# A graph layer's edge kernel: 52 instead of 42 edge tiles loaded row by row, half of each from ScalarE, and the result's rows sent a slot later

## The chip, the core and the metric

The kernel runs on one core of a Trainium2 chip. The metric is the device time of one launch in microseconds (us). The core's engines run their own instruction queues in order and wait for each other by semaphores: TensorE (PE), VectorE (DVE), ScalarE (ACT), GpSimd (POOL) and SyncE (SP). SyncE, ScalarE and GpSimd also start DMA transfers from their queues, in the order of the program.

## What is computed

One message-passing layer over 6250 nodes with 128 features and 206250 directed edges sorted by receiver, then a residual and a normalization. In float32, cut to what matters:

```python
def layer(node_feats, edge_feats, chi, cutoffs, senders, receivers):
    w = silu(edge_feats @ rad_W1 + rad_b1) @ rad_W2 + rad_b2       # 32 -> 128 -> 128
    w = w + silu(chi @ sph_W1 + sph_b1) @ sph_W2 + sph_b2
    q = (node_feats @ Wq)[receivers]; k = (node_feats @ Wk)[senders]
    v = (node_feats @ Wv)[senders]                                 # 8 heads of 16
    alpha = (q * w * k).sum(per head) / sqrt(16) * cutoffs
    return segment_sum(alpha * v, receivers) / 16
out = layernorm(x + layer(x, ...))
```

## The kernel before

**Tiles.** Edges are taken 128 at a time (a tile, one edge per partition). Four tiles make a quad (512 edges), four quads a group; there are 403 quads in 101 groups. The list `order` gives the quads of a group in the order 0, 2, 1, 3. The main loop makes one step per quad, called a slot here; `slot` runs from 0 to 3 in each group `g`, and `i` counts all slots. The program is one written order per engine: each engine works through its calls as the loop makes them.

**Set-up.** The keys and values of all nodes are computed once and stored as a table `kv_tab` (one row of 1 KB per node). The first ten quads don't use the table: their senders' features are gathered from x and multiplied. Meanwhile indices, receivers and biases are prepared.

**A slot.** On TensorE: small products of the group (`turn_q`, `make_q`, `sum_group`, lines 249 to 661), the sums of the group before (`sum_quads`, L616), the first layer of the quad after next (`first_layers`, L518), the queries at the edges of the next quad (`q_at_edges`, L527), and its second layer (`weigh`, L560 and L565). On ScalarE: the two silus of the quad after next (`silus`, L548), each held back by a mark of TensorE so that it does not run ahead, and one small copy out of PSUM (L253, L260, L652 or L661). On VectorE: query times key for the next quad (`multiply`, L577), and for the present one the product with the weights (L585), the sum per head (L587), the cutoff (L591) and the messages (L604). Per group VectorE also makes the one-hot matrices, of which `hotT` (L264) needs the receivers' indices `relb`; these are loaded by SyncE two groups ahead, in slot 2 (`load_rel`, L235), next to the edge features (`load_feats`, L224). `load_x` (L283) loads a piece of x in slot 0.

**Keys and values of an edge tile** come in one of two ways. Most tiles are fetched by GpSimd with one indirect DMA each (`gather`, L132), 14 quads ahead of their use into a ring of 16 buffers; a gather is held back by the mark of a quad of TensorE 14 quads earlier. In 42 quads, spread evenly from slot 20 to slot 392 (`row_at`), the fourth tile is instead loaded row by row into a buffer `wide` (three of them): 128 transfers of 1 KB, each with its address in a register. SyncE sends 80 of these rows in units of 32, 32 and 16: a register load (L186) and then a burst of rows (L191). ScalarE sends 48 in two units of 24, spread out: two rows between the two silus of a slot and up to four at its end. A register load of ScalarE stands at the end of a slot and takes the place of one row there. The window of a tile ends eight slots ahead of its use (`ROW_LEAD`). VectorE waits for a tile's rows in front of L577 (`multiply`), and handles the quad in two pieces, three tiles and one.

**The result.** Every fourth group, at the end of slot 3, `statistics` normalizes four pieces (ScalarE, L682 to L696, which needs another activation table and then silu's again) and puts them on a list `written`. `write_rows` (L708) in each slot sends one piece of the list from SyncE's queue, beginning with slot 0 of the next group. Pieces overlap in rows, so each write waits for the one before to land.

Of the kernel before, what the change touches and what calls it, by code (L numbers as in the profile page):

```python
# [35 lines left out]
NG = math.ceil(E / (P * GT))  # L36
# [9 lines left out]
ROW_BYTES = 2 * D * 4  # L46
XQ = 10
RING = 16
ROW_TILES = 42
ROW_FIRST = 20  # L50
ROW_LAST = 392
ROW_LEAD = 8
ROW_UNIT = 32
ROW_ACT = 48
ROW_UNIT_ACT = 24
ROW_SLOT_ACT = 6
ROW_SEMS = 8
CHECK = 20
XL = 3
# [6 lines left out]
def gnn_kernel(ctx, tc, x, src, dst, weight, edges, rad_W1, rad_b1, rad_W2, rad_b2,  # L66
# [26 lines left out]
    src_x = const.tile([P, math.ceil(XQ / NQ) * GT], I32, name="src_x")  # L93
    at_i = const.tile([ROW_TILES, P], I32, name="at_i")
    scale = const.tile([P, NT], F32, name="scale")
# [32 lines left out]
    def quad_of(name, bufs, width=D):  # L128
        return ep.tile([P, QT, width], F32, name=name, bufs=bufs)
# [8 lines left out]
    order = [g * NQ + j for g in range(NG) for j in (0, 2, 1, 3) if g * NQ + j < QUADS]  # L138
    row_at = [ROW_FIRST + (n + 1) * (ROW_LAST - ROW_FIRST) // ROW_TILES for n in range(ROW_TILES)]
    row_quads = {order[i] for i in row_at}  # L140
    row_of = {}
    row_done = {}
    act_rows, act_now = [], []
    row_sems = [tc.alloc_semaphore(f"rows_{n}") for n in range(ROW_SEMS)]
    row_count = [0] * ROW_SEMS

    def next_rows(n):
        for _ in range(min(n, len(act_now))):
            act_now.pop(0)()

    def rows_at_end():
        n = ROW_SLOT_ACT - 2
        m = min(n, len(act_now))
        next_rows(m)
        if not act_now and act_rows:
            f, e, r = act_rows.pop(0)
            act_now.extend(f(e, r))
            next_rows(n - m - 1)

    r_of = {}  # L160
    feats_of, relb_of, act_of, kv_of, hot_of, hotT_of, x_of, q_of, msg_of = ({} for _ in range(9))
# [11 lines left out]
    def load_rows(i):  # L173

        k = next((k for k in range(ROW_TILES) if i <= row_at[k] - ROW_LEAD), None)
        start = len(order) if k is None else (row_at[k - 1] if k else ROW_FIRST) - ROW_LEAD + 1
        if i < start:
            return rows_at_end() if k is None else None
        q = order[row_at[k]]
        n = P - ROW_ACT  # L180
        slots, units = row_at[k] - ROW_LEAD + 1 - start, math.ceil(n / ROW_UNIT)
        a, b = ((j * units + slots - 1) // slots for j in (i - start, i - start + 1))
        table = kv_tab.bitcast(U8).rearrange("(o n) b -> o (n b)", o=1)

        def registers(e, m, engine):
            return nc.values_load_multi_w_load_instructions(  # L186
                at_i[k:k + 1, e:e + m], engines=(engine,), min_val=0,
                max_val=(N - 1) * ROW_BYTES, skip_runtime_bounds_check_because="senders are nodes")[1]

        def one_row(engine, p, r):  # L190
            return engine.dma_start(row_of[q][p:p + 1, 0, :].bitcast(U8), table[:, ds(r, ROW_BYTES)])  # L191

        def rows_of_act(first, m):
            rows = registers(first, m, ACT)
            for p in range(m):
                yield lambda p=p: signalled(one_row(nc.scalar, first + p, rows[p]))

        def signalled(o):
            tc.no_tile_sem_insts.add(o.ins.name)
            tc.add_to_no_dep_group(f"rows_{q}", o.ins)  # L200
            o.then_inc(row_sems[k % ROW_SEMS], 16)
            row_count[k % ROW_SEMS] += 16
            row_done[q] = row_sems[k % ROW_SEMS], row_count[k % ROW_SEMS]

        if i == start:
            row_of[q] = quad_of("wide", 3, P)[:, :2, :].rearrange("p t d -> p (t d)")[:, None, :]
        for e in range(a * ROW_UNIT, min(min(b, units) * ROW_UNIT, n), ROW_UNIT):
            m = min(ROW_UNIT, n - e)
            rows = registers(e, m, SP)
            for p in range(m):  # L210
                signalled(one_row(nc.sync, e + p, rows[p]))
        if i == start:
            act_rows.extend((rows_of_act, e, min(ROW_UNIT_ACT, P - e)) for e in range(n, P, ROW_UNIT_ACT))
        rows_at_end()

    def kv_parts(q, t):

# [55 lines left out]
    def rows_from(table, at):  # L273

        return table.bitcast(U8).rearrange("n b -> (n b)")[ds(at, P * D * 4)].rearrange(
            "(p b) -> p b", p=P)
# [30 lines left out]
    with tc.tile_pool(name="nodes", bufs=1) as nodes, \  # L307
# [76 lines left out]

        rows_f = nodes.tile([P, ROW_TILES], F32, name="rows_f")

# [6 lines left out]
        def turn_rows():  # L393
            pt = nps.tile([P, QT, P], F32, name="pt", bufs=3)
            nc.tensor.transpose(pt[:ROW_TILES, 0, :], rows_f, ident)
            nc.vector.tensor_copy(at_i, pt[:ROW_TILES, 0, :])

# [64 lines left out]
        n = len(chunks)  # L462
# [49 lines left out]
    with tc.tile_pool(name="ps", bufs=1, space=PSUM) as pp:  # L512
# [192 lines left out]
        def write_rows(n=1):  # L705
            for _ in range(min(n, len(written))):
                g, y = written.pop(0)
                nc.sync.dma_start(rows_from(out, r_of.pop(g)), y.bitcast(U8))  # L708
# [16 lines left out]
        def verdict():  # L725

            pe = pp.tile([P, D], F32, name="po")
            nc.tensor.matmul(pe[:1, :8], ones[:, :1], ends, start=True, stop=True)
            found = gp.tile([1, 1], F32, name="found")
            nc.vector.tensor_reduce(found, pe[:1, :8], AX.X, OP.add)  # L730
            nc.vector.tensor_scalar(general, found, 0.0, None, op0=OP.is_gt)

        written = []
# [9 lines left out]
        multiply(order[0])  # L743
        marks = weigh(order[0])
        mark = marks[-1]
        for g in range(NG - 1):
            for slot, j in enumerate((0, 2, 1, 3)):
                q = g * NQ + j
                i = g * NQ + slot
                turned, past, old = None, mark, marks  # L750
                if slot == 0 and g == CHECK + len(checks) + 1:
                    verdict()
                if slot == 0:
                    turned = turn_q(g + 1, pp.tile([P, EQ], F32, name="pq", bufs=2))
                if slot == 1 and 2 <= g:
                    turned = sum_group(g - 2)
                if slot == 2:
                    turned = make_q(g + 1, pp.tile([P, EQ], F32, name="pq", bufs=2))
                if 1 <= g:
                    for t in ((), (0, 1), (2,), (3,))[slot]:  # L760
                        mark = sum_quads(g - 1, t)
                first_layers(order[i + 2])
                mark = q_at_edges(order[i + 1])
                marks = weigh(order[i + 1])
                silus(order[i + 2], mark, marks, lambda: next_rows(2))
                if turned:
                    turned()
                if 1 <= g and slot == 3:
                    part_sums(g - 1)
                if i + AHEAD < len(order):  # L770
                    gathers(order[i + AHEAD], old[-QT:])
                multiply(order[i + 1], mark)
                messages(q, scores(q, marks=marks), marks=marks)
                if slot == 0:
                    if g + XL < NG:
                        load_x(g + XL, past)
                if slot == 2:
                    if g + 3 < NG:
                        load_feats(g + 3, past)
                    if g + 2 < NG:  # L780
                        load_rel(g + 2)
                if slot == 1:
                    one_hots_T(g + 1)
                    if g + 2 < NG:
                        pick(g + 2)
                    if 1 <= g:
                        place(g - 1)
                write_rows()
                if slot == (3 if g < NG - 2 else 2):
                    if 2 <= g:  # L790
                        statistics(g - 2)
                if slot == 3:
                    if g + 1 < NG - 1:
                        one_hots(g + 1)
                    if CHECK <= g < CHECK + len(checks):
                        checks[g - CHECK]()
                if g == NG - 3 and slot in (0, 2):
                    wide_one_hots(order[slot // 2 - 3])
                if g == NG - 2 and slot == 0:
                    wide_one_hots(order[-1])  # L800
                    n = nc.values_load(general, min_val=0, max_val=1)
                    place(g)
                    place(NG - 1)
                if g == NG - 3 and slot in (1, 3):
                    weigh_wide(order[slot // 2 - 3])
                if g == NG - 2 and slot == 1:
                    weigh_wide(order[-1])
                load_rows(i)
# [206 lines left out]
```

## Time and profile before

| | |
|---|---|
| median of 3 runs | 1985.04 us (1985.03 to 1985.54) |
| profiled execution | 1985.41 us |
| its span, first to last instruction | 1983.3 us |
| granted TensorE clock, mean | 0.916 |
| instructions | 55295 |
| GpSimd gathers of kv_tab | 1530 |
| rows sent by SyncE / ScalarE | 3360 / 2016 |

The span leaves 2.1 us of the profiled execution outside. In the lines of the profile each group of instructions has its line, engine and operation, the tensors out<-in, and the count behind an x; behind the first bar stand the busy time (us) and the mean of one (ns), behind the second the engine's idle time in front of them and who ended it. In a timeline a row is start, duration, engine, line, operation and count, with the idle time in front of it in brackets. Busy time of a queue that only issues DMAs (SPq, ACTq) isn't in the busy shares of the engines. A row of windows has the window, its length, the busy time of each engine asked for (with the count of instructions), and at the end the granted clock, the busy share of the DMA engines and GB/s.

### The profile page before, as it was taken

The page shows a single profiled execution, that of the slowest core. Times are in us where ns is not written, and L with a number is a line of the kernel's source. Part 1 is how long each engine was busy: PE and PEld are TensorE (multiplying, and loading weights), DVE is VectorE, ACT ScalarE, POOL GpSimd, SP SyncE. Part 2 cuts the span into 40 slices and gives each one's busy share as a digit, 9 for nine tenths or more (in the row PEclk, how much of TensorE's full clock was granted, in tenths as well). Part 3 has the DMA queues.
Part 4 walks back from the last instruction along what each step waited for, and adds up shares of the span by engine and source line. Part 5 has one row for each costly group of instructions (what it writes and reads, how often), then busy time and mean ns, then how long its engine had stood idle before and what let it go on. Part 6 is the DMA issues. An engine that isn't in the chain of part 4 may idle for free.

```text
span 1983.3 us, 55295 instructions
## 1 busy us (share of the span) xinstructions
PE 1782.5 (90%) x16014; PEld 1505.7 (76%) x16014; DVE 1471.1 (74%) x3123; ACT 752.2 (38%) x1437; POOL 1488.6 (75%) x1580
## 2 busy tenths in 40 slices
PE   9899999978997988998898888899989988898897
PEld 7788788767876877876787777777767777777786
DVE  6687777768876877776777777767767767777777
ACT  3244344333343343342343333333433433433334
POOL 7777777777777777777777777777777777777775
PEclk9899899978998998998999889989989999898988
DMA  8545545455455555454554555545545455445543
GB/s 316 160 141 156 157 145 156 142 157 156 143 157 154 146 156 154 144 160 139 159 158 140 159 142 155 158 143 154 154 145 158 144 152 159 142 142 158 157 140 90
DMA packets 150194, 304.77 MB, mean 154 GB/s; under 512 B 38732, under 2 KB 83900, under 8 KB 149884
## 3 DMA queue, kind: packets, MB, share of 16 engines
q0 software_dynamic: 74720, 203.26, 36.7%
q1 hardware_dynamic: 69632, 95.45, 14.8%
q10 hardware_dynamic: 5532, 2.47, 0.5%
q8 instruction: 128, 2.10, 0.4%
q14 instruction: 182, 1.49, 0.3%
HBM read 287.58 MB, written 13.46 MB: 152 GB/s over the span
## 4 chain that ended last, share of the span: by engine, by line
PE 56%; DMA 17%; DVE 11%; issue 6%; POOL 3%; ACTq 2%; SPq 2%; ACT 2%; DVEq 0%; POOLq 0%
PE pw L565 28%; DMA kv<-kv_tab,src_i 14%; PE pq L527 10%; PE ph L518 7%; PE po L616 4%; DVE kq L577 4%; DMA relb<-rel_lin 3%; PE pw L560 3%; ACTq L191 2%; POOL msg L132 2%; DVE side L587 2%; DVE kq L585 2%; SPq L191 1%; PE pq L657 1%; POOL kv L132 1%
## 5 line engine op out<-in xcount | busy, mean ns | idle before, releaser
L132 POOL DMA_INDIRECT kv<-kv_tab,src_i x1530 | 1447.9, 946 | 466.6 <-PE pw L565 174.2
L548 ACT ACTIVATE act<-ph,b 128x512 f32<-128x512 f32 x806 | 546.5, 687 | 1091.0 <-PE pq L527 1003.5
L565 PEld LDWEIGHTS pw<-w,act 128*128 128x128 f32 x6448 | 822.8, 207 | 105.6 <-issue 94.7
L565 PE MATMUL pw<-w,act 128*128 128x128 f32 x6448 | 902.7, 298 | 0.0
L527 PE MATMUL pq<-q,hotT 32*128 32x128 f32 x3224 | 502.9, 299 | 50.8 <-DVE hotT L264 40.4
L518 PE MATMUL ph<-feats,w 32*128 32x512 f32 x1612 | 501.2, 680 | 31.5 <-ACT act L548 30.6
L527 PEld LDWEIGHTS pq<-q,hotT 32*128 32x128 f32 x3224 | 422.8, 200 | 75.9 <-issue 55.4
L577 DVE TENSOR_TENSOR kq<-pq,kv 128x512 f32<-128x512 f32 (+1 forms) x403 | 271.8, 674 | 243.8 <-PE pq L527 121.2
L587 DVE TENSOR_REDUCE side<-kq 128x32 f32<-128x512 f32 x403 | 280.1, 695 | 43.2 <-DVE kq L585 1.4
L604 DVE TENSOR_TENSOR msg<-kv,side 128x512 f32<-128x512 f32 (+1 forms) x404 | 271.9, 673 | 42.7 <-DVE side L591 1.2
L585 DVE TENSOR_TENSOR kq<-pw,kq 128x512 f32<-128x512 f32 x403 | 274.7, 682 | 0.0
L518 PEld LDWEIGHTS ph<-feats,w 32*128 32x128 f32 x1612 | 137.9, 193 | 113.7 <-issue 58.2
L560 PE MATMUL pw<-brow,onesb 3*128 3x512 bf16 x403 | 161.9, 402 | 9.4 <-DVE kq L585 9.3
L616 PE MATMUL po<-msg,hot 128*32 128x128 f32 x3200 | 154.6, 290 | 0.0
L264 DVE TENSOR_TENSOR hotT<-relb,side 128x512 f32<-128x512 bf16 x101 | 69.0, 683 | 97.5 <-DMA relb<-rel_lin 97.4
L657 PE MATMUL pq<-part,to 128*128 128x128 f32 x200 | 45.9, 313 | 82.6 <-DVE kq L577 58.0
L591 DVE TENSOR_TENSOR side<-side,scale 128x32 f32<-128x32 f32 x400 | 80.0, 200 | 42.3 <-DVE side L587 0.5
L657 PEld LDWEIGHTS pq<-part,to 128*128 128x128 f32 x200 | 31.3, 197 | 93.0 <-issue 54.0
L616 PEld LDWEIGHTS po<-msg,hot 128*32 128x32 f32 x3200 | 71.3, 111 | 38.3 <-issue 4.8
L269 DVE TENSOR_TENSOR hot<-rel,side 128x512 f32<-128x512 f32 x100 | 66.1, 661 | 0.0
L258 PE MATMUL pq<-wq,xT 128*128 128x128 f32 x200 | 42.9, 299 | 11.2 <-DVE kq L577 11.1
L132 POOL DMA_INDIRECT msg<-in_x,src_x x40 | 38.9, 972 | 13.3 <-issue 11.6
(117 smaller groups left out, 855.6 us busy)
## 6 DMA issues: line engine op xcount, KB each, us to landing
wide<-kv_tab SPq DMA_DIRECT2D x3360, 1.0 KB
feats<-in_edges SPq DMA_DIRECT2D x101, 512.0 KB
wide<-kv_tab ACTq DMA_DIRECT2D x2016, 1.0 KB
kv<-kv_tab,src_i POOLq DMA_INDIRECT x1530
relb<-rel_lin SPq DMA_DIRECT2D x101, 128.0 KB
x<-in_x SPq DMA_DIRECT2D x101, 64.0 KB
out<-y SPq DMA_DIRECT2D x101, 64.0 KB
kv_tab<-kv SPq DMA_DIRECT2D x12, 512.0 KB
```

Source lines behind the costliest of these rows:

```text
L132: return nc.gpsimd.indirect_dma_start(out=o, out_offset=None, in_=table, in_offset=bass.IndirectOffsetOnAxis(ap=index, axis=0))
L518: return nc.tensor.matmul(act_of[q, i], w1[r0:r0 + R, :], feats_of[g][r0:r0 + R, c0:c0 + EQ], start=True, stop=True)
L527: o = nc.tensor.matmul(pq_of[q][:, t, :], hotT_of[g][b, t * P:(t + 1) * P], q_of[g][b, :], start=True, stop=True)
L548: o = nc.scalar.activation(act, act_of[q, i], AF.Silu, bias=b1[:, i:i + 1])
L560: nc.tensor.matmul(pw, onesb, brow.rearrange("p t d -> p (t d)"), start=True, stop=False)
L565: o = nc.tensor.matmul(pw[:, t, :], act_of[q, i][:, t * P:(t + 1) * P], w2[:, i, :], start=False, stop=(t == QT - 1 and i == 1))
L577: o = nc.vector.tensor_tensor(kq_of[q][:, u, :], pq_of[q][:, u, :], kv[:, :, :D], op=OP.mult)
L585: nc.vector.tensor_tensor(m, pw_of[q][:, t, :], m, op=OP.mult)
L587: o = nc.vector.tensor_reduce(alpha, m.rearrange("p t (h e) -> p t h e", e=HD), AX.X, OP.add)
L604: o = nc.vector.tensor_tensor(msg_of[q][:, u, :].rearrange("p t (h e) -> p t h e", e=HD), kv[:, :, D:].rearrange("p t (h e) -> p t h e", e ...
L616: o = nc.tensor.matmul(po_of[g][j * W:(j + 1) * W, :], hot_of[g][:, j * QT + t, :], msg_of[g * NQ + j][:, t, :], start=(t == 0), stop=(t = ...
L657: nc.tensor.matmul(ph[:, :D], to[:n, 0, :], part[:n, :], start=True, stop=(g == 0))
```

## The change

The fourth tile of 52 quads is loaded row by row, over the same stretch of slots, so one quad in 7.15 has such a tile instead of one in 8.86. Each of the two engines sends 64 rows of a tile in two units of 32. ScalarE still sends two rows between the silus; at the end of a slot it now sends as many as bring it to an even share of the tile's rows over the slots of its window, and loads registers when it runs out of them, however many rows that makes. `write_rows` sends a piece only if the list already held something when the slot before had sent its own, so the first piece goes out in slot 1 instead of slot 0; the last two groups are as before.

```diff
-ROW_TILES = 42
+ROW_TILES = 52
...
-ROW_ACT = 48
-ROW_UNIT_ACT = 24
-ROW_SLOT_ACT = 6
+ROW_ACT = 64
+ROW_UNIT_ACT = 32
...
+    act_sent = [0]
 
     def next_rows(n):
         for _ in range(min(n, len(act_now))):
             act_now.pop(0)()
-
-    def rows_at_end():
-        n = ROW_SLOT_ACT - 2
-        m = min(n, len(act_now))
-        next_rows(m)
-        if not act_now and act_rows:
-            f, e, r = act_rows.pop(0)
-            act_now.extend(f(e, r))
-            next_rows(n - m - 1)
+            act_sent[0] += 1
+
+    def rows_at_end(goal):
+        while act_sent[0] < goal:
+            if not act_now:
+                f, e, r = act_rows.pop(0)
+                act_now.extend(f(e, r))
+            next_rows(min(len(act_now), goal - act_sent[0]))
...
         if i < start:
-            return rows_at_end() if k is None else None
+            return
...
-        rows_at_end()
+        rows_at_end(k * ROW_ACT + ROW_ACT * (i - start + 1) // slots)
...
         mark = marks[-1]
+        made_before = 0
         for g in range(NG - 1):
...
-                write_rows()
+                write_rows(1 if made_before or g >= NG - 2 else 0)
+                made_before = len(written)
```

## The prediction

> **What bounds the kernel now.** I began with busy time and the costliest groups, where GpSimd (POOL) looks a quarter idle.
>
> ```profile
> PE 1782.5 (90%) x16014; PEld 1505.7 (76%) x16014; DVE 1471.1 (74%) x3123; ACT 752.2 (38%) x1437; POOL 1488.6 (75%) x1580
> L132 POOL DMA_INDIRECT kv<-kv_tab,src_i x1530 | 1447.9, 946 | 466.6 <-PE pw L565 174.2
> DMA  8545545455455555454554555545545455445543
> ```
>
> It is not idle. 1447.9 + 466.6 = 1914.5 us, and 1914.5 / 1530 = 1.251 us per gather: 0.946 busy and 0.305 in front of it. The timeline of POOL at both ends shows that this gap is the same everywhere, whoever is named behind the arrow, so it belongs to the gather and is no wait for work.
>
> ```profile
> 52.87 0.94 POOL L132 DMA_INDIRECT msg<-in_x,src_x  x1 [0.30 <-issue]
> 54.12 1.03 POOL L132 DMA_INDIRECT kv<-kv_tab,src_i  x1 [0.30 <-DVE b_all L379]
> ```
>
> ```profile
> 1966.14 0.94 POOL L132 DMA_INDIRECT kv<-kv_tab,src_i  x1 [0.30 <-PE pw L565]
> 1967.39 0.94 POOL L132 DMA_INDIRECT kv<-kv_tab,src_i  x1 [0.30 <-issue]
> ```
>
> From 54.12 to 1968.33 POOL issues one gather behind the other; 1983.3 - 1968.3 = 15.0 us of tail follow. So the span is 54.1 + 1914.2 + 15.0. TensorE must keep up with this. How the two stand to each other I read from the windows of line 560 (one bias product opens each quad) and of line 132:
>
> ```profile
> 0.00:110.00 110.00, 4.40 (x11) 1.01 (x11) 0.94 0.69 226
> 110.00:980.00 870.00, 75.01 (x188) 17.46 (x188) 0.92 0.52 151
> 1020.00:1890.00 870.00, 72.70 (x180) 16.63 (x180) 0.92 0.52 151
> ```
>
> ```profile
> 0.00:110.00 110.00, 81.34 (x85) 0.94 0.69 226
> 110.00:980.00 870.00, 658.02 (x696) 0.92 0.52 151
> ```
>
> At 110 us POOL has done 45 kv gathers (85 less the 40 of x), which with the ten quads that need none makes about 21 quads; TensorE has begun 11. It starts ten quads behind, goes on at 870/188 = 4.63 us a quad, POOL feeds one per 4.86 (four gathers less a tenth), and near 980 TensorE has caught up. From there it is held at 870/180 = 4.83. The waits of VectorE before and after 980 us (two answers) say what holds it in each half:
>
> ```profile
> DVE hotT L264 <- DMA relb<-rel_lin: 82.1, 21, 12.3
> ```
>
> ```profile
> DVE kq L577 <- DMA kv<-kv_tab,src_i: 83.5, 54, 3.7
> DVE hotT L264 <- DMA relb<-rel_lin: 15.3, 5, 7.6
> ```
>
> First half: the receivers' load (relb), late because SyncE (SP) is behind; second half: the gathers. The end is set by the gathers alone.
>
> **The change part by part.** *Ten gathers fewer.* A tile loaded singly takes one gather off POOL. 52 - 42 = 10, times 1.251 us, is 12.5 us off a queue without slack: 1985.41 - 12.5 = 1972.9 for the profiled execution, 1985.04 - 12.5 = 1972.5 for the median, which lies 0.4 below it. Nothing late moves in behind, if TensorE keeps the new pace. It has 392 quads to begin between 110 us and where its last one may start:
>
> ```profile
> 1970.75 0.38 PE L560 MATMUL pw<-brow,onesb 3*128 3x512 bf16 x1
> ```
>
> To begin there 12.5 us earlier it may take (1958.2 - 110)/392 = 4.715 us a quad on its own; break-even is (1970.7 - 110)/392 = 4.747. It has 4.63 now, so 0.085 a quad, 33 us in all, may be lost before the gain shrinks, and 46 before it is gone. All other terms are weighed against these two.
>
> *ScalarE's queue* gets 3328 rows for 2016, and 104 register loads of 32 for 84 of 24. Per slot that is 64/7.15 = 8.9 rows instead of 5.4: two between the two silus as before, about seven behind instead of four. What stands behind them on the queue is the next quad's first silu; TensorE waits for that at the next first layer (line 518).
>
> ```profile
> 698.79 0.69 ACT L548 ACTIVATE act<-ph,b 128x512 f32<-128x512 f32 x1 [2.22 <-PE pq L527]
> 699.52 0.69 ACT L548 ACTIVATE act<-ph,b 128x512 f32<-128x512 f32 x1
> 700.26 0.55 ACTq L191 DMA_DIRECT2D wide<-kv_tab  x2
> 701.10 0.70 PE L518 MATMUL ph<-feats,w 32*128 32x512 f32 x2
> 701.63 0.59 PE L518 MATMUL ph<-feats,w 32*128 32x512 f32 x2
> 702.40 0.69 ACT L548 ACTIVATE act<-ph,b 128x512 f32<-128x512 f32 x1 [2.02 <-PE pq L527]
> 708.53 0.23 ACTq L191 DMA_DIRECT2D wide<-kv_tab  x1
> ```
>
> A row takes 0.55 - 0.23 = 0.32 us. In this slot, one of the short ones (3.6 us), the queue is done at 700.81 and the next silu comes at 702.40: 1.6 us to spare. Three more rows leave 0.65, so the ordinary slot costs nothing. A slot with a register load is another matter:
>
> ```profile
> L186 SPq TENSOR_LOAD <-at_i x126: 979/1924/2497, 122.9 to 1877.2; - x126
> L186 ACTq TENSOR_LOAD <-at_i x84: 1662/1780/2070, 127.0 to 1871.1; - x84
> ```
>
> ScalarE's 24 took 1.78; 32 did not occur there. Bounds: 1.8, and SP's longest (its 32s) 2.5. Scaled by 32/24 it is 2.4, which I take, with 0.2 for a first row behind it: 0.65 - 2.6 makes the silus 1.95 us late. First layers start 701.10 - 699.48 = 1.6 us behind the first silu's end, and the second pair 701.63 - 700.21 = 1.4 behind the second's, so TensorE loses about 0.55. Short slots are the rule; three silus in a row:
>
> ```profile
> 682.39 0.69 ACT L548 ACTIVATE act<-ph,b 128x512 f32<-128x512 f32 x1 [1.99 <-PE pq L527]
> 686.00 0.69 ACT L548 ACTIVATE act<-ph,b 128x512 f32<-128x512 f32 x1 [2.03 <-PE pq L527]
> 689.51 0.69 ACT L548 ACTIVATE act<-ph,b 128x512 f32<-128x512 f32 x1 [1.94 <-PE pq L527]
> ```
>
> They lie 3.6 and 3.5 us apart. I take three of a group's four slots (the one of the statistics is longer) to be that short while the clock is full; a mean clock of 0.92 with halves means full for about 0.83 of the time. 104 x 0.75 x 0.83 = 65 slots, 36 us. Bounds: nothing, if loads fall on long slots, and 104 x 0.65 = 68.
>
> *The statistics slots.* There rows stand between the normalizing and the reload of silu's table.
>
> ```profile
> 707.89 0.55 ACTq L191 DMA_DIRECT2D wide<-kv_tab  x2
> 708.99 0.48 ACT L696 ACTIVATE y<-y,shift,rs 128x128 f32<-128x128 f32 x1
> 709.49 1.28 ACT L548 ACT_TABLE_LOAD   x1
> 711.52 1.80 PE L518 MATMUL ph<-feats,w 32*128 32x512 f32 x2 [1.13 <-ACT act L548]
> ```
>
> TensorE already waits here, so lateness counts in full. Seven rows end at 707.83 + 7 x 0.32 = 710.1 instead of 709.1, past the last normalizing at 709.47: 0.6 us. With a load and seven to nine rows it is 3.2 to 3.8. In the changed kernel's queue 23 such slots carry rows, 7 of them a load (now 5, with fewer rows, worth about 1.3 each): 16 x 0.6 + 7 x 3.4 - 5 x 1.3 = 27 us; bounds 10 and 45.
>
> *SP's queue.* 64 rows per 7.15 slots instead of 80 per 8.86: 8.95 a slot for 9.03, still in bursts.
>
> ```profile
> 677.52 0.55 SPq L235 DMA_DIRECT2D relb<-rel_lin  x1
> 680.68 10.73 SPq L191 DMA_DIRECT2D wide<-kv_tab  x32
> 692.17 0.37 SPq L283 DMA_DIRECT2D x<-in_x  x1
> ```
>
> One burst with its load holds the queue from 678.1 to 691.4, nearly four short slots, so what queues behind (x, features, relb) comes late as now. The result's rows wait in the same queue; SP's waits in 100 to 980 us and TensorE's share of the relb waits there (two answers):
>
> ```profile
> SPq L708 <- DMA out<-y: 56.8, 22, 4.8
> SPq L708 <- ACT y L696: 5.4, 2, 5.0
> ```
>
> ```profile
> PE pq L527 <- DVE hotT L264: 35.6, 9, 9.2
> ```
>
> Two writes stood together ahead of a group's relb, the second waiting 56.8/22 = 2.6 us for the first to land. One slot later only one stands ahead; the pair, and its wait, moves behind relb, ahead of x and a burst. So relb gains 0 to 2.6 us in each of some 25 groups, and SP's total falls by nothing to 62 us in that half. I take part of it: relb no later than now.
>
> *Sum for TensorE.* 36 + 27 = 63 us over 392 quads is 0.16, so 4.79 if every relb wait stayed. But those waits are SP being slower than TensorE: 35.6/188 = 0.19 a quad at a pace of 4.63, and hardly any at 4.83 (15.3 us after 980, where SP had the same rows to send). What ScalarE adds takes their place first. With none left it is 4.60, with half of them 4.69; both are under 4.715. One more thing speaks for the second half of this exchange: the row of a long wait, and the window of all engines around it (granted clock: the third number from the end).
>
> ```profile
> 614.28 0.69 DVE L264 TENSOR_TENSOR hotT<-relb,side 128x512 f32<-128x512 bf16 x1 [10.30 <-DMA relb<-rel_lin]
> ```
>
> ```profile
> 614.00:618.00 4.00, 2.88 (x11) 2.36 (x12) 3.50 (x8) 0.69 (x1) 3.09 (x4) 0.50 0.55 129
> ```
>
> Behind the wait the clock is half, so a wait costs more than its length. The Trainium skill (TensorE: Matmul & The Clock Gate, Part 1) says that an idle window of about 3.4 us halves the matrix clock until a busy one has passed; the trace agrees, with 0.50 granted in the window right behind a 10.30 us wait for relb.
>
> *Small things.* All rows of a tile are still sent eight slots ahead of its use, so VectorE's wait for them stays met. VectorE does two products in two pieces for ten more tiles: twenty more instructions in an engine that is a quarter idle. Ten more one-column products and ten more rows of a transpose fall in the set-up, under TensorE's lag of ten quads: nothing.
>
> **Rivals.** (1) *Gathers still set the end:* 1972.5. For it: no slack anywhere on POOL. (2) *TensorE keeps part of the gain:* 4.715 to 4.747 a quad, 1972.5 to 1985; half of the relb waits stay and ScalarE costs its middle value or a little more. (3) *ScalarE's queue becomes the bound, slower:* the late silus of the load and statistics slots cost 63 us and the relb waits stay, since SP still sends bursts of 32. 4.79 x 392 + 110 = 1988 for the last quad instead of 1970.7: 17 us more, 2002. It decides from 46 us of new waits on. Against it: the two kinds of wait replace one another. (4) *No change:* the DMA engines are the limit, and it doesn't matter who sends the bytes. Then 1985. The busy share of 0.52 in the windows above, and gathers that start every 1.25 us whatever else flows, speak against it. The Trainium skill (DMA: Bandwidth & Descriptors, Issuing engines are not separate DMA queues) says just this of bandwidth, and that other issuers save only issue time; here issue time on POOL is what is short.
>
> **How the numbers follow.** (1) 0.77, (2) 0.08, (3) 0.12, (4) 0.03. Predicted: 1972.5. Its own range is 1970.5 to 1976: 2 us either way for how TensorE stands to the last gathers in the tail, a little more above for a denser row traffic. To hold 8 in 10 it takes in about half of (2): 1970.5 to 1981. A measurement here tells 0.2%, 4 us, from nothing. Faster: (1) and most of (2), 0.84; same: (4) and the end of (2), 0.04; slower: (3), 0.12.
>
> **What would show it.** Right: 1520 gathers still 1.25 us apart, the last one ending near 1956, the tail 15 us; relb waits smaller in total, a longer total of "PE ph from ACT act", kv waits of VectorE still in the second half. Wrong: gaps of more than 0.31 us in front of gathers (POOL waiting for TensorE's marks, which lie 14 quads back), TensorE never reaching the gathers and no kv waits at the end, or hotT waits above 100 us.

## The result: slower, 2003.2 us instead of 1985.0

The changed kernel takes 2003.16 us (median of 5 runs, 2001.40 to 2008.36) against 1985.03 for the kernel before on the same chip (1984.36 to 1985.54): a ratio of 1.0095, 95% interval 1.0081 to 1.0110. The prediction was 1972.5, faster. The profiled execution took 2001.40 us; its page begins (in the changed file the lines behind `ROW_ACT` stand one lower than before: L132 is now L131, L560 is L559, and so on):

```profile
span 1999.6 us, 57805 instructions
PE 1812.9 (91%) x16014; PEld 1516.8 (76%) x16014; DVE 1471.7 (74%) x3153; ACT 747.8 (37%) x1437; POOL 1479.0 (74%) x1570
```

The busy shares hardly differ from before. What differs stands in the costliest groups and at the end of the timeline of GpSimd, and then of TensorE:

```profile
L131 POOL DMA_INDIRECT kv<-kv_tab,src_i x1520 | 1438.5, 946 | 464.2 <-PE pw L564 172.0 <-issue 154.4 <-DMA kv<-kv_tab,src_i 63.5
...
1955.24 0.95 POOL L131 DMA_INDIRECT kv<-kv_tab,src_i  x1 [0.30 <-issue]
...
1986.60 0.38 PE L559 MATMUL pw<-brow,onesb 3*128 3x512 bf16 x1
```

Ten gathers fewer, still (1438.5 + 464.2) / 1520 = 1.252 us apart, the last one done at 1956.2: this half of the forecast came true to half a microsecond. But the last quad's bias product starts at 1986.60, where 1958.2 was needed, and POOL has long been done. From 110 us on TensorE needed (1986.6 - 110) / 392 = 4.787 us a quad. The windows of that product show the pace in both halves (the number in the first brackets of a row is the count of quads):

```profile
110.00:980.00 870.00, 72.12 (x180) 16.86 (x180) 0.92 0.53 150
1020.00:1890.00 870.00, 71.82 (x179) 16.87 (x179) 0.92 0.53 151
```

870/180 = 4.83 in the first, where it was 4.63, and 4.86 in the second, now without ever reaching the gathers. The clock is the same 0.92, and the DMA engines' busy share is 0.53 for 0.52. What VectorE, TensorE and SyncE wait for, in the whole run, first before:

```profile
DVE hotT L264 <- DMA relb<-rel_lin: 97.4, 26, 12.3
DVE kq L577 <- DMA kv<-kv_tab,src_i: 85.9, 58, 3.7
...
PE ph L518 <- ACT act L548: 30.6, 22, 2.6
...
SPq L708 <- DMA out<-y: 122.7, 50, 5.5
```

Then in the changed kernel (SyncE's row follows below):

```profile
DVE hotT L263 <- DMA relb<-rel_lin: 121.3, 29, 10.9
PE ph L517 <- ACT act L547: 93.4, 80, 5.0
...
DVE kq L576 <- DMA kv<-kv_tab,src_i: 10.7, 13, 1.3
```

The kv waits that marked the gathers as the bound (85.9 us in all before) are nearly gone. The waits for silus grew from 30.6 us to 93.4. The waits for relb grew from 97.4 to 121.3. SyncE's own list has what is in front of relb on its queue:

```profile
SPq L707 <- DMA out<-y: 195.8, 56, 11.4
```

Before, SyncE waited 122.7 us in 50 waits for a written piece to land, so that the next piece may follow; the longest was 5.5. In 100 to 980 us alone it is 87.6 for 56.8. One such wait in SyncE's timeline:

```profile
423.37 10.85 SPq L190 DMA_DIRECT2D wide<-kv_tab  x32
434.32 0.37 SPq L223 DMA_DIRECT2D feats<-in_edges  x1
434.80 0.57 SPq L234 DMA_DIRECT2D relb<-rel_lin  x1
435.54 10.67 SPq L707 DMA_DIRECT2D out<-y  x2
446.93 0.35 SPq L282 DMA_DIRECT2D x<-in_x  x1
```

The first write of the pair goes out at 435.54, behind the 512 KB of edge features and relb. A transfer's landing is told by sixteen signals. The trace has fifteen of this write's: fourteen of them were there at 440.54, the last came at 445.75. SyncE stood still for 9.8 us and sent nothing.

**SyncE is the bound.** To see it, SyncE's time between the bias products of quads 10 and 200 is divided among its instructions (sums of their durations with the gaps under 0.15 us behind them, by 190 quads; us a quad):

```
                        before  changed  old writes  one write  few ScalarE rows  56/72 rows
pace of TensorE          4.648   4.790     4.788       4.617         4.590          4.682
rows sent                2.921   2.883     2.863       2.914         2.895          2.540
register loads for rows  0.629   0.606     0.605       0.591         0.616          0.544
waits at the writes      0.327   0.531     0.548       under 0.02    0.286          0.463
waits for TensorE        0.052   0.040     0.041       0.394         0.061          0.392
```

(The four columns on the right are experiments below.) Before, SyncE had 0.05 us a quad to spare in this half; in the changed kernel 0.04. What the rows leave of the pace, 0.72 to 0.74 us in every column, are SyncE's other loads. From before to changed the rows and loads fall by 0.06 as forecast, the waits at the writes rise by 0.20, and the pace by 0.14, which is their sum. In the second half (quads 200 to 385) the changed kernel goes on at 4.840.

### The profile page after: what moved, and what is told of

It reads as the page before. It is cut to its first block, busy times and chain, and to the rows that moved or that the text cites. A ratio compares the mean times of both kernels' runs of the same rounds, so it can differ in the third digit from the quotient of the medians.

```text
span 1999.6 us, 57805 instructions
## 1 busy us (share of the span) xinstructions
PE 1812.9 (91%) x16014; PEld 1516.8 (76%) x16014; DVE 1471.7 (74%) x3153; ACT 747.8 (37%) x1437; POOL 1479.0 (74%) x1570
## 2 busy tenths in 40 slices
DMA packets 152294, 304.94 MB, mean 152 GB/s; under 512 B 39852, under 2 KB 86300, under 8 KB 151964
## 4 chain that ended last, share of the span: by engine, by line
PE 60%; ACTq 9%; issue 8%; DMA 7%; DVE 7%; ACT 6%; POOL 2%; SPq 1%; DVEq 0%; POOLq 0%
PE pw L564 29%; PE pq L526 11%; PE ph L517 11%; ACTq L190 7%; ACT act L547 4%; DMA relb<-rel_lin 4%; PE po L615 4%; DMA kv<-kv_tab,src_i 3%; PE pw L559 2%; ACTq L185 2%; POOL msg L131 2%; DVE kq L576 2%; DVE side L586 1%; DVE kq L584 1%; PE pq L257 1%
## 5 line engine op out<-in xcount | busy, mean ns | idle before, releaser
L131 POOL DMA_INDIRECT kv<-kv_tab,src_i x1520 | 1438.5, 946 | 464.2 <-PE pw L564 172.0
L517 PE MATMUL ph<-feats,w 32*128 32x512 f32 x1612 | 552.8, 666 | 95.0 <-ACT act L547 93.4
L526 PE MATMUL pq<-q,hotT 32*128 32x128 f32 x3224 | 497.0, 296 | 59.2 <-DVE kq L576 59.0
L526 PEld LDWEIGHTS pq<-q,hotT 32*128 32x128 f32 x3224 | 417.4, 198 | 76.0 <-issue 75.2
L517 PEld LDWEIGHTS ph<-feats,w 32*128 32x128 f32 x1612 | 159.5, 191 | 218.6 <-ACT act L547 160.6
L559 PE MATMUL pw<-brow,onesb 3*128 3x512 bf16 x403 | 161.0, 400 | 0.0
L263 DVE TENSOR_TENSOR hotT<-relb,side 128x512 f32<-128x512 bf16 x101 | 69.0, 683 | 121.4 <-DMA relb<-rel_lin 121.3
L131 POOL DMA_INDIRECT msg<-in_x,src_x x40 | 38.6, 966 | 13.3 <-issue 11.6
```

The lines of the kernel that those rows point to most:

```text
L131: return nc.gpsimd.indirect_dma_start(out=o, out_offset=None, in_=table, in_offset=bass.IndirectOffsetOnAxis(ap=index, axis=0))
L517: return nc.tensor.matmul(act_of[q, i], w1[r0:r0 + R, :], feats_of[g][r0:r0 + R, c0:c0 + EQ], start=True, stop=True)
L526: o = nc.tensor.matmul(pq_of[q][:, t, :], hotT_of[g][b, t * P:(t + 1) * P], q_of[g][b, :], start=True, stop=True)
L559: nc.tensor.matmul(pw, onesb, brow.rearrange("p t d -> p (t d)"), start=True, stop=False)
```

## Experiments

Every ratio is against runs of the kernel before on the same chip. The first eight ran on chips where that kernel takes 1988.6 (the first four) and 1984.7 us (the next four).

**Writes in their old place.** Is it the slot by which the writes were put off?

```diff
-                write_rows(1 if made_before or g >= NG - 2 else 0)
+                write_rows()
```

> The changed kernel with the result's rows sent as before (first piece in slot 0). Theory A (SyncE: the second write of a pair now waits behind features and relb, so relb comes late): SyncE's waits for out fall from 196 us to about 125, VectorE's relb waits from 121 us to 80 or less, and the time to 1978-1988. Theory B (ScalarE: late silus behind the added rows and register loads): relb waits may fall, but the first layer's waits for silu rise above their 93 us instead, and the time stays at 1997-2003.

Measured: 2003.26 us, ratio 1.0064 (1.0047 to 1.0081). SyncE's waits at the writes and VectorE's for relb:

```profile
SPq L707 <- DMA out<-y: 182.0, 54, 6.8
SPq L707 <- ACT y L695: 62.8, 11, 26.2
```

```profile
DVE hotT L263 <- DMA relb<-rel_lin: 133.2, 35, 11.3
```

The theory that the new place of the writes is the cause falls. Back in front of relb the writes wait as long for each other to land: 0.51 us a quad in the stretch of the table above, for 0.50 in the changed kernel and 0.30 before. For ScalarE they wait 0.04 to 0.05 in all three. The ratio is 0.3% below the changed kernel's, but so much slower was the kernel before on this chip, and the changed kernel wasn't run on it: a gain of that size is not excluded.

**One write a group.** Pieces of the result go out four slots apart, so that none waits for the one before.

```diff
-                write_rows(1 if made_before or g >= NG - 2 else 0)
+                write_rows(1 if slot == 2 or g >= NG - 6 else 0)
```

> The changed kernel with one piece of the result sent per group, in slot 2 behind relb (each slot again in the last five groups), so that no write finds the one before still under way. Theory A: SyncE's waits for out under 30 us, relb waits under 40 us, time 1972.5-1978 (the gathers' bound). Theory B: 1993-2003, the first layer's waits for silu at 93 us or more.

Measured: **1978.19 us, ratio 0.9949 (0.9932 to 0.9965)**, faster than both kernels. The waits of SyncE, TensorE and VectorE in this run:

```profile
SPq L707 <- DMA out<-y: 22.9, 9, 6.0
...
PE ph L517 <- ACT act L547: 83.6, 69, 5.0
...
DVE kq L576 <- DMA kv<-kv_tab,src_i: 93.8, 61, 6.7
```

The writes' waits are nearly gone, the relb waits wholly (they are no longer in VectorE's list), and the kv waits are back: the gathers set the end. ScalarE's late silus are nearly as many as in the changed kernel, 83.6 us. So they alone don't cost the gain; the theory that ScalarE's queue is the bound falls with this run.

**ScalarE's rows as two transfers.** The 64 rows of each tile that ScalarE sends become two transfers of 32 fixed rows, sent at the start of the tile's window (`next_units` sends all that is listed); the bytes are the same, the data are not the senders' rows.

```diff
...
-            rows = registers(first, m, ACT)
-            for p in range(m):
-                yield lambda p=p: signalled(one_row(nc.scalar, first + p, rows[p]))
+            yield lambda: signalled(nc.scalar.dma_start(
+                row_of[q][first:first + m, 0, :], kv_tab[first:first + m, :]))
...
-        rows_at_end(k * ROW_ACT + ROW_ACT * (i - start + 1) // slots)
+        if i == start:
+            next_units()
```

> The changed kernel with ScalarE's 64 single rows of a tile and their register loads replaced by two transfers of 32 fixed rows of the table (so these edges get wrong keys and values); SyncE as in the changed kernel. Theory A: SyncE stays late, relb waits stay at 100 us or more, time 1992-2003. Theory B: the first layer's waits for silu fall to 20 us or less and the time to 1972.5-1980.

Measured: 1973.99 us, ratio 0.9928 (0.9911 to 0.9945). The silu waits of TensorE and SyncE's waits at the writes:

```profile
PE ph L523 <- ACT act L553: 17.6, 22, 2.5
...
SPq L713 <- DMA out<-y: 96.1, 41, 5.6
```

Not only ScalarE's part falls, from 93.4 to 17.6. The waits of SyncE for its writes halve too, though SyncE's own list of work is untouched.

**SyncE's rows as two transfers.** The same for SyncE's 64 rows.

```diff
-            rows = registers(e, m, SP)
-            for p in range(m):
-                signalled(one_row(nc.sync, e + p, rows[p]))
+            signalled(nc.sync.dma_start(row_of[q][e:e + m, 0, :], kv_tab[e:e + m, :]))
```

> The changed kernel with SyncE's 64 single rows of a tile and their register loads replaced by two transfers of 32 fixed rows (these edges get wrong keys and values); ScalarE as in the changed kernel. Theory A: relb waits vanish, time 1972.5-1980. Theory B: relb waits vanish too, but the late silus remain and the time stays above 1988.

Measured: 1974.21 us, ratio 0.9931 (0.9914 to 0.9947).

```profile
PE ph L515 <- ACT act L545: 85.5, 65, 5.0
...
DVE kq L574 <- DMA kv<-kv_tab,src_i: 99.3, 62, 6.8
```

With SyncE relieved, 85.5 us of late silus remain and the gathers set the end all the same. This is the second run against ScalarE as the bound.

**56 rows from SyncE, 72 from ScalarE.** A theory formed from these runs: SyncE is full, and whatever takes work or waits off it helps, at ScalarE's cost if need be.

```diff
-ROW_ACT = 64
-ROW_UNIT_ACT = 32
+ROW_ACT = 72
+ROW_UNIT_ACT = 24
```

> The changed kernel with 56 rows of a tile from SyncE and 72 (three loads of 24) from ScalarE. Theory S (SyncE is full, and its work per slot, waits for out included, sets the pace): eight rows fewer per 7.15 slots take 0.36 us off SyncE's 4.79 us a slot, so the gathers bound again: 12 us below the kernel before, about 0.994 of it, relb waits under 60 us. Theory B (ScalarE's late silus cost TensorE directly): more rows on ScalarE, slower than the changed kernel, 1.010 of the kernel before or more.

Measured: 1980.22 us (1973.47 to 1981.47), ratio 0.9970 (0.9954 to 0.9986).

```profile
PE ph L517 <- ACT act L547: 137.2, 111, 4.8
...
1958.14 0.38 PE L559 MATMUL pw<-brow,onesb 3*128 3x512 bf16 x1
```

The silu waits grow to 137.2 us, 44 more than in the changed kernel, and yet the ratio is 0.9970 instead of 1.0095. In the profiled run (1973.47) the last quad starts at 1958.14, just where ten gathers fewer needed it.

**ScalarE's loads in units of 16.** Shorter loads, so shorter lateness for each.

```diff
-ROW_UNIT_ACT = 32
+ROW_UNIT_ACT = 16
```

> The changed kernel with ScalarE's registers loaded in four units of 16 instead of two of 32, so that no slot gets more than about 1.2 us of load. Theory S: the first layer's waits for silu fall to about half, but SyncE's waits for out and relb's lateness stay: 1.004 to 1.010 of the kernel before. Theory B: the time falls with those waits, to 1.000 or less.

Measured: 1999.83 us, ratio 1.0072 (1.0057 to 1.0086).

```profile
PE ph L517 <- ACT act L547: 69.9, 41, 4.0
...
SPq L707 <- DMA out<-y: 187.6, 56, 11.1
...
DVE hotT L263 <- DMA relb<-rel_lin: 137.0, 27, 12.7
```

The silu waits fall by 23.5 us, the relb waits rise by 15.7, the time stays within 4 us. While SyncE is full, a wait taken from ScalarE's side comes back at relb.

**The kernel before with one write a group.** The edit of the second experiment, made in the kernel before.

> The kernel before (42 tiles) with one piece of the result sent per group, in slot 2. Theory S: SyncE gets idle time, relb waits fall from 97 us to under 20, the first half runs faster, but the gathers set the end: 0.999 to 1.001. If relb waits had cost time in the kernel before: 0.997 or less.

Measured: 1986.23 us, ratio 1.0008 (0.9994 to 1.0022).

```profile
SPq L708 <- DMA out<-y: 11.6, 7, 2.2
...
DVE kq L577 <- DMA kv<-kv_tab,src_i: 163.1, 96, 4.5
```

SyncE's waits are nearly gone here too, and VectorE waits longer for the gathers instead (163.1 us for 85.9). Fewer writes in a row are worth nothing by themselves, and the ten gathers fewer, as the change makes them, cost 1%; together they are worth half a per cent.

**58 tiles with one write a group.** Six gathers fewer again.

```diff
-ROW_TILES = 52
+ROW_TILES = 58
```

> 58 tiles, 64 and 64 rows, one piece of the result per group. Theory S: SyncE's work is 4.26 us a slot at 52 tiles with this and rises by 0.4 to 4.7, still under the gathers' 4.81: six gathers fewer, 7.5 us below the kernel with 52 tiles and one write a group, 0.991 of the kernel before. If SyncE or ScalarE bind first: 0.995 or more, with relb waits back above 60 us.

Measured: 2025.47 us, ratio 1.0202 (1.0187 to 1.0217). It is not SyncE this time: its waits for writes are 22.1 us. The gathers of GpSimd are no longer evenly spaced:

```profile
391.77 0.95 POOL L131 DMA_INDIRECT kv<-kv_tab,src_i  x1 [0.30 <-DMA kv<-kv_tab,src_i]
...
400.53 0.95 POOL L131 DMA_INDIRECT kv<-kv_tab,src_i  x1 [0.30 <-issue]
403.93 0.95 POOL L131 DMA_INDIRECT kv<-kv_tab,src_i  x1 [2.45 <-PE pw L564]
405.21 0.94 POOL L131 DMA_INDIRECT kv<-kv_tab,src_i  x1 [0.33 <-issue]
```

104 starts lie over 1.4 us apart (two in the changed kernel), which adds 63 us. Gathers signal on eight semaphores in turn, and in such a gap GpSimd waits for the one of the gather eight before. The gather at 403.93 is eight behind the one at 391.77, which had fifteen of its sixteen landing signals at 395.21 and the sixteenth at 403.17, 0.76 us ahead of that start. (The arrow names TensorE, whose mark only came last by the profile.) In 90 of the 104 gaps the gather starts 0.76 or 0.79 us behind the last signal of the one eight before, and never sooner; what ended the others isn't clear. Eight gathers take 10 us; a landing near that holds up the next.

**What makes the sixteenth signal late.** Over all gathers whose signals are complete in the trace, the time from the end of the issue to the fifteenth and the sixteenth signal (means, us):

```
                        single rows  fifteenth  sixteenth
before                     5376        2.31       2.82
before, one write          5376        2.29       2.83
changed                    6656        2.32       4.10
one write a group          6656        2.31       4.21
56/72 rows                 6656        2.28       4.07
58 tiles                   7424        2.32       6.31
few ScalarE rows           3328        2.24       2.47
few SyncE rows             3328        2.15       2.44
```

Fifteen signals come alike everywhere; the last one depends on how many rows are sent singly. The result's writes show the same between 100 and 980 us, counted from the start of their issue: the fifteenth signal at 2.72 us before and 2.46 in the changed kernel, the sixteenth at 3.13 and 4.22, and at 3.32 with few ScalarE rows (means of the 22 to 27 writes whose signals are complete). So it is the last signal that makes SyncE wait longer, not all the traffic. A single row is one packet of 1 KB in the trace. ScalarE's packets pile up: matched in their order, a row's packet starts 1.32 us behind its issue before, 2.64 in the changed kernel and 5.48 with 58 tiles (medians). In the changed kernel 1404 of the 3328 start within 0.2 us of the one before, closer than their issues at 0.32, and only 8 overlap the one before in time; as two transfers of 32 rows the same 3328 packets do so 3029 times. So single rows of a queue come one behind the other, as on a single DMA engine. The Trainium skill (DMA: Bandwidth & Descriptors, Why a DMA increments its semaphore by 16 and not by 1) says that a transfer started by SyncE or ScalarE is spread over as many engines as its outermost dimension above one allows, up to sixteen and always the lowest-numbered ones, so that one undivided row would always meet the same engine. The trace agrees as far as it shows: 8 overlaps for 3029, and a sixteenth signal that falls from 4.10 to 2.47 us with the same bytes in wider transfers. Which engine it is no trace here names.

**Rows in pieces.** To test this by itself, a row was divided into four pieces of 256 bytes (with 52 tiles, with 58, and with one write a group), and into two halves that lie apart in SBUF (with 52 tiles and with 58). The edit for the four pieces:

```diff
-            return engine.dma_start(row_of[q][p:p + 1, 0, :].bitcast(U8), table[:, ds(r, ROW_BYTES)])
+            o = row_of[q][p:p + 1, 0, :].bitcast(U8).rearrange("p (k b) -> p k b", k=ROW_PARTS)
+            return engine.dma_start(o, table[:, ds(r, ROW_BYTES)].rearrange("o (k b) -> o k b", k=ROW_PARTS))
```

> The changed kernel with one edit: each single row goes as 4 pieces of 256 bytes instead of one of 1024; same rows, same queues, same order, same number of issues. Theory E (single rows of one piece all run on one and the same DMA engine, which then finishes its share of every other transfer late): the sixteenth landing of a gather falls from 4.1 us after issue to about 2.5 (mean), SyncE's waits for the result's writes fall from 196 to 90-140 us, its slot in the first half from 4.79 to about 4.70, and the time to 1975-1985. Rival D (the writes land late because of all the traffic, or because of their place in the queue, whichever engine carries a row): the sixteenth landing and the waits stay, 2000-2004. Rival I (a transfer of four pieces takes longer to issue than 0.32 us): SyncE's rows take longer per slot and the time is above 2005.

> 58 tiles loaded singly, one write of the result a group, and each row as 4 pieces of 256 bytes. Theory E: the engine that made gathers wait for their slowest landing (16th landing 6.3 us on average, 207 of them over 8 us, 104 gaps of over 1.4 us between gathers) is relieved; the gathers are 1.25 us apart again, and with 1514 of them the time is 1966-1975, set by the gathers or by TensorE with about 93 us of waits for silu. Rival D: gaps stay, 2020-2028. Rival I: slower still, above 2030.

> 52 tiles, one write of the result a group, and each row as 4 pieces of 256 bytes. With rows of one piece this version was set by the gathers (1978). Theory E: the gathers were evenly spaced already, so the time hardly changes: 1972-1979; SyncE has more idle time. Rival D: the same time. Rival I: SyncE, which had 0.36 us a slot to spare, gets slower by more than that and the time goes over 1985.

> The changed kernel with one edit: each single row is written as two halves of 512 bytes that lie apart in SBUF, so that a transfer has two pieces that cannot be joined; same rows, same number of issues, same order. Theory E (a single row runs on one DMA engine, always the same, which finishes its share of every other transfer late): with two pieces that engine has half of the bytes; the sixteenth landing of a gather falls from 4.1 us after issue to 3.5 or less, SyncE's waits for the result's writes from 196 to 110-170 us, the time to 1978-1998. Rival D (the lateness comes from all the traffic, or from the place in the queue): landing, waits and time stay, 2000-2005. Rival I (two pieces take longer to issue than one): SyncE's 0.32 us a row grows, and the time is above 2005.

> 58 tiles loaded singly, one write of the result a group, and each row in two halves of 512 bytes that lie apart. Theory E: the sixteenth landing of a gather falls from 6.3 us (mean) to under 5, fewer than 60 gaps of over 1.4 us between gathers instead of 104, and the time from 2025 to 1970-2010. Rival D: 2020-2028. Rival I: above 2028.

These are lost for the question, for two reasons. The chips that ran them were others, on which the kernel before takes 2626 to 2664 us with a granted clock near 0.82: with rows in one piece TensorE sets the pace there, and SyncE and the gathers wait for it. And the four pieces were joined again: the run has 152294 packets, as many as the changed kernel. So its 2670.29 us, a ratio of 1.0170 (1.0135 to 1.0205), should be the changed kernel's on such a chip; with one write a group it is 1.0154 (1.0124 to 1.0184), with 58 tiles 1.0403 (1.0371 to 1.0436). Halves that lie apart stay two packets, but cost more to issue, the outcome of the third theory: 3860.07 us (ratio 1.4484, 1.4438 to 1.4530), and 4145.07 with 58 tiles (1.5574, 1.5514 to 1.5634). Rows of SyncE in two pieces, and of the next experiment's kernel on the same chip in one:

```profile
599.49 23.16 SPq L191 DMA_DIRECT2D wide<-kv_tab  x28
```

```profile
600.68 13.18 SPq L190 DMA_DIRECT2D wide<-kv_tab  x29
```

A row's issue on SyncE has a median of 0.562 us instead of 0.228, and 23.16 / 28 = 0.83 us from row to row for 0.45. VectorE waits 990.8 us for relb in this run. One sign agrees with the theory: from 110 us on ScalarE's 6656 half rows overlap the packet before 1582 times, where the 3328 whole rows of the run with joined pieces do so twice.

**The changed kernel with 42 tiles; one write a group with 54.** The first changes nothing but the number of tiles and so would show what the ten tiles' rows alone do to the writes.

```diff
-ROW_TILES = 52
+ROW_TILES = 42
```

> The changed kernel with 42 tiles loaded singly instead of 52; 64 rows of each from SyncE, 64 from ScalarE over the slots, and the result's rows two slots behind, all as changed. Nothing is gained at the gathers, 1985 is the least. If the ten tiles' rows are what makes the writes wait: SyncE's rows per slot fall by a fifth, its waits for writes to under 120 us, and the gathers set the end at 1985. If the shift of the writes or ScalarE's new order were the cause: above 1990.

> 54 tiles loaded singly and one write of the result a group. Two gathers fewer than with 52 tiles are worth 2.5 us if the gathers stay 1.25 us apart: a ratio of 0.9935 where 52 tiles gave 0.9949. If the landing of the gathers already runs up to the eighth gather ahead, as at 58 tiles (1.0202), gaps of over 1.4 us appear (more than ten) and the ratio is 0.995 to 1.005.

(The shift of the result's rows that the first of these names is one slot, not two.)

All runs fell on chips of the second kind: with 42 tiles 1.0029 (1.0014 to 1.0045), and again 1.0062 (1.0044 to 1.0080) and 1.0033 (1.0018 to 1.0048); with 54 tiles 1.0187 (1.0159 to 1.0215) and 1.0172 (1.0148 to 1.0196). On such a chip GpSimd waits for TensorE (the gathers' row and its longest wait, with 42 tiles):

```profile
L131 POOL DMA_INDIRECT kv<-kv_tab,src_i x1530 | 1445.6, 945 | 1101.3 <-PE pw L564 489.2 <-issue 340.5 <-remote 221.3
...
POOL kv L131 <- PE pw L564: 489.2, 275, 23.2
```

So they can't show what binds where SyncE is full. SyncE's waits for its writes to land were 70 to 77 us here with 42 tiles, and 68 in the run with 52 and joined pieces: where a slot takes a third longer, the ten tiles' rows don't lengthen them. The runs do show that on such chips the loss grows with the number of single-row tiles: 0.3 to 0.6% at 42, 1.5 to 1.9% at 52 and 54, 4.0% at 58. Why was not found.

## Why the prediction was wrong

- *Ten gathers fewer, 12.5 us off POOL's queue:* right. The last gather ended at 1956.2 (forecast: near 1956), with a period of 1.252 us. Where SyncE is relieved the gain shows: with one write a group the gathers bind again and the ratio is 0.9949 (0.9932 to 0.9965), where 1972.5 / 1985.04 = 0.9937 was forecast.
- *The limits of 4.715 and 4.747 us a quad:* right. The changed kernel needed 4.787 and was slower; the profiled run with 56/72 rows began its last quad at 1958.14, which is 4.715, and took 1973.5 us.
- *63 us of new waits on ScalarE's queue:* right in sum; its two terms, 36 and 27, weren't measured apart. "PE ph from ACT act" rose from 30.6 to 93.4, by 62.8. A load of 32 registers took 2.21 us in the median, estimated at 2.4. But they don't decide: 83.6, 85.5 and 137.2 us of them stood in kernels that reached the gathers or nearly did.
- *"What ScalarE adds takes their place first":* the first step that failed. In the first half the relb waits of VectorE did fall, from 82.1 to 58.5 us, but that was far from half, and after 980 us they rose from 15.3 to 62.9. The prediction took SyncE's rate as fixed, so that SyncE would catch up with a slower TensorE. But SyncE, with 0.05 us a quad to spare before, became slower itself.
- *"SP's total falls by nothing to 62 us", "relb no later than now":* the second step, and the cause of the first. The part about rows was right: SyncE's rows and loads fell from 3.55 to 3.49 us a quad. The term that was wrong is what the waits at the writes cost, forecast to stay or to fall: 0.33 us a quad before, 0.53 after, 195.8 us of landing waits in all for 122.7. They were taken to be a fixed 2.6 us each that moves with the writes; in the changed kernel one takes 195.8 / 56 = 3.5 us on average, for 122.7 / 50 = 2.5. The old place of the writes gives the same total, so the shift is not to blame.
- *"gathers that start every 1.25 us whatever else flows", and the DMA engines' busy share of 0.52 (against rival 4):* too coarse. The share was 0.53, and the gathers stayed 1.25 us apart at 52 tiles; but the mean over sixteen engines doesn't show a single late signal, the sixteenth, 2.82 us before and 4.10 after. And the time of a queue was short on SyncE too, not only on POOL, with SyncE's time going into waits between its issues.
- *Rival 3, 2002 us:* its number came out (profiled 2001.4; 4.787 a quad for its 4.79) by a coincidence of parts. It kept the relb waits and added ScalarE's. The runs show that the pace is SyncE's, 4.648 plus 0.20 at the writes less 0.06 of rows; ScalarE's late silus lie beside that, as the runs with 8 rows shifted to ScalarE and with loads of 16 show. What was said against it, that one kind of wait replaces the other, is true (the loads of 16 show it), only with SyncE as the one that keeps its length.
- *What would show it wrong:* "TensorE never reaching the gathers and no kv waits at the end, or hotT waits above 100 us" is what the trace shows: 10.7 and 121.3.

Shown: SyncE bounds the changed kernel, and its waits at the writes are what took the gain and more (the writes spread out give it back; their place leaves the landing waits as they are; ScalarE's waits alone don't take the gain), and these waits grew because a write's last signal comes later, 4.22 us for 3.13, with more rows sent singly. Supported, but not shown by itself: that the last signal is late because single rows keep one DMA engine behind. The rows' packets that pile up without overlap and the runs with wider transfers agree with it (0.29 us a quad at the writes for 0.53), but the latter change the rows' issue too, and those that were to divide a row were lost. Open: how many tiles between 52 and 58 are best with one write a group.

## What to carry to other kernels

A queue that only issues DMAs has no busy share in the profile; sum its issues, register loads and waits per loop step before giving it work or a new neighbour, and count a wait for a landing by what shares the DMA engines with it, not by its length before. If two transfers must follow each other, put a whole loop group between them rather than let the queue stand still for the first to land. Moving work off the bound (ten gathers, 12.5 us) pays only if the next bound, here SyncE with 0.05 us a step to spare, has room.

## What the runs showed of the hardware

- Many single-row transfers go with a late last signal of other transfers: the sixteenth signal of a gather came at 2.82 us with 5376 such rows, 4.10 with 6656 and 6.31 with 7424, the fifteenth always near 2.3; the mean busy share of the DMA engines stayed at 0.51 to 0.53. The writes' sixteenth came at 3.13 us with 5376 and 4.22 with 6656.
- GpSimd's gathers wait for the landing of the gather eight before. With 7424 rows there were 104 gaps, up to 3.3 us for the usual 0.30, and 90 of them ended 0.76 or 0.79 us behind that gather's last signal.
- A row in two pieces that lie apart takes 0.562 us to issue, in one 0.228; four adjoining pieces become one again (152294 packets in the run, as in the changed kernel).
- The kernel before took 1985 to 1989 us on some chips and 2626 to 2664 on others, with a granted clock of 0.92 and 0.82. The clock's 0.92 / 0.82 = 1.12 doesn't cover 2626 / 1985 = 1.32; the rest is open. The changed kernel lost 1.0% on one kind and, in the run with joined pieces, 1.7% on the other.
